# Batch 0's layer-norm statistics taken by VectorE, and the sums over the attention weights folded into one matrix product per chunk

## The chip, the cores and the metric

The kernel runs on one core of a Trainium2 chip. A core has a matrix engine (TensorE, "PE" in the profile, with its weight loads listed as "PEld"), a vector engine (VectorE, "DVE"), an activation engine (ScalarE, "ACT"), a general engine (GpSimd, "POOL") and a queue engine (SyncE, "SP"), each with its own instruction stream, which it works through in order; they wait for one another on semaphores. Sixteen DMA engines move data between the device memory and the on-chip memory; their transfers are issued from the SP, ACT and POOL streams. The metric is the device time of one execution in microseconds (us).

## The reference

The input `x` has 4 batches of 512 time steps (tokens), each with 128 x 64 = D = 8192 features. A first layer does linear attention, a convolution over the 128 frequencies, a causal convolution over time and a feed-forward network, each behind a layer norm over all 8192 features; a second layer does a spectral convolution over time. Only the beginning of the first layer matters here:

```python
xn = layernorm(x.reshape(b, t, d), ln_attn_g, ln_attn_b)
k = xn @ Wk
v = xn @ Wv
r = jax.nn.sigmoid(xn @ Wr)
decay = jnp.exp(-jnp.exp(w_decay))
kv = jnp.swapaxes(k * v, 0, 1)
...                                   # s = decay * s + kv, over time
attn = r * states @ Wo
x = x + attn.reshape(b, t, f, h)
xn = layernorm(x.reshape(b, t, d), ln_freq_g, ln_freq_b)...
```

`Wk`, `Wv`, `Wr` are 8192 x 64 and `Wo` is 64 x 8192. With g and b the weights of the first layer norm, mean m and inverse deviation s of a token, k = s (x (g Wk) - m (g . Wk)) + b . Wk: the product can run on raw x, and be corrected afterwards with the token's two statistics and with the column sums g . W and b . W of the weights. The statistics of the second layer norm, of x + attn, can also be had without a second pass over x: they need the 64 row sums of Wo (Wo times a vector of ones), the 64 x 64 matrix Wo Wo^T and the cross product x Wo^T.

## The kernel before

**Tiling.** x is held in two forms in device memory: feature-major `xt` (64 chunks of 128 features by 512 tokens) and token-major `x`. The 64 chunks are worked on in 32 pairs. `wkvr` holds, for each chunk, 128 rows of 256 numbers: the columns of Wk, Wv, Wr and Wo^T, 64 each.

**Stages.** For each batch the first layer runs `project` (k, v, r and x Wo^T summed over all chunks in PSUM), `scan` (corrections, the recurrence over time, and the second norm's statistics), `attend_and_convolve`, `convolve_time`, `open_feed` and `feed_forward`. The calls at the end of `layer0` set their order: `project(0)` runs alone, then `prepare()`, which folds constants, and then `in_turn` weaves two chains of stages into each other step by step (`scan(0)` and `attend_and_convolve(0)` with `project(1)` and `scan(1)`, and so on). TensorE's instructions stand in exactly this written order. For the other engines and for the SP stream, a scheduler that models the run chooses the order, and the instructions then wait for each other on semaphores; a stream never overtakes its own waiting instruction.

**`project`.** A pair takes one load of `wkvr` (line 333, 256 KB), one of `xt` (line 292, tile `xp`, 512 KB), a scaling of the three projection weights by g on VectorE (line 358, twice), and four products of 128 x 128 weights with 128 x 512 inputs (line 361). The two kinds of batch differ:

- Batch 0 (lines 336 to 348) has six small products per pair that add up g . W, b . W, Wo Wo^T and the sums of Wo (lines 341 to 343, with a column of ones that GpSimd writes at line 336). Its token statistics come from TensorE: ScalarE squares `xp` (line 345), and `add_up` (line 249) multiplies `xp` and its square, one pair late, by columns of ones. Its weights lie in the buffers called `x1` (three of them), which the attention uses later.
- Batches 1 to 3 (lines 351 to 355) load the same part of x a second time, token-major (512 KB per pair), and take the statistics from it with VectorE's `bn_stats`, two of 128 x 512 per pair. Weights and token-major data share the two buffers `wx`.

**`scan`.** Batch 0 turns the TensorE sums into columns (`finish`, lines 257 to 266), the other batches use `bn_aggr`. Then GpSimd computes the inverse deviation (`rsqrt`, lines 230 and 231), TensorE spreads mean and inverse deviation over the partitions (`rows`, line 239, copied by ScalarE at line 283), and a chain of VectorE work with single products between (lines 427 to 465) gives the gated state `rst`. Batch 0 also duplicates its weight sums over the two halves of the partitions (lines 402 to 418). In batch 0 the tile `kv` is one of the `x1` buffers.

**Buffers.** `xp` has three, `x1` three, `z` four, `wx` two. PSUM tiles (`a`, `c`, `m`, `p`, `s`) have one buffer each. `spare` is a small helper that allots one of these on-chip tiles by its tag.

Of the kernel before, what the change touches and what calls it, by code (L numbers as in the profile page):

```python
# [16 lines left out]
P = 128  # L17
# [62 lines left out]
def layer0(ctx, tc, dram, x, xt, vecs, wkvr, wo, wdec, wconv, fbias, w1, fb1, w2, fb2, x4):  # L80
# [209 lines left out]
    def load_x(b, i):  # L290
        xp = fr.tile([P, 2, SL], F32, tag="xp", name="xp")
        nc.sync.dma_start(xp, xt[b, 2 * i : 2 * i + 2].rearrange("c p t -> p c t"))
        return xp

    def c_bank():
        return two(ps_c, "c")
# [14 lines left out]
    free_s = [True]  # L311
    held = [False]


    def project(b):
        pa = two(ps_m, "m") if b == 1 else two(ps_a, "a")
        held[0] = b == 1
        if b == 0:
            psum_w = two(ps_m, "m")
            psum_q = ps_p.tile([P, SL], F32, tag="p", name="psum_q")  # L320
            st = ps_s.tile([P, SL], F32, tag="s", name="st")
        else:
            stt = rowp.tile([P, NT, NS, 6], F32, tag="stt", name="stt")
        waiting = None
        for i in range(NPR):
            first, last = i == 0, i == NPR - 1
            if b == 0:
                wq = two(fr, "x1")[:, :, 0 : 4 * S + 1]
            else:

                both = fr.tile([P, 2, 4 * S + SL], F32, tag="wx", name="both", bufs=2)
                wq, xk = both[:, :, 0 : 4 * S], both[:, :, 4 * S :]
            nc.sync.dma_start(wq[:, :, 0 : 4 * S], wkvr[2 * i : 2 * i + 2].rearrange("c p s -> p c s"))
            xp = load_x(b, i)
            if b == 0:
                nc.gpsimd.memset(wq[:, :, 4 * S :], 1.0)
                for j in range(2):
                    c = 2 * i + j
                    at = dict(start=c == 0, stop=c == NCH - 1)
                    w = wq[:, j, :]  # L340
                    nc.tensor.matmul(psum_w[:, 0, 0:2], lhsT=w[:, 0:P], rhs=vec[:, G1 : B1 + 1, c], **at)
                    nc.tensor.matmul(psum_w[0:S, 1, 0:2], lhsT=w[:, P : P + S], rhs=vec[:, G1 : B1 + 1, c], **at)
                    nc.tensor.matmul(psum_q[S:P, 0 : S + 1], lhsT=w[:, P + S : P + 2 * S], rhs=w[:, P + S :], **at)
                sq1 = bk.tile([P, 2, SL], F32, tag="sq", name="sq1")
                nc.scalar.activation(sq1, xp, AF.Square)
                if waiting is not None:
                    add_up(st, *waiting, i == 1, False)
                waiting = i, xp, sq1
            else:
                s, h = i // 2, i % 2 * 2  # L350
                nc.sync.dma_start(
                    xk, x[b, h * P : (h + 2) * P, s * SL : (s + 1) * SL].rearrange("(t p) d -> p t d", p=P)
                )
                for t in range(2):
                    nc.vector.bn_stats(stt[:, h + t, s, :], xk[:, t, :])  # L355
            for j in range(2):
                w = wq[:, j, 0 : 3 * S]
                nc.vector.tensor_scalar_mul(w, w, vec[:, G1, 2 * i + j : 2 * i + j + 1])  # L358
            for j in range(2):
                for k in range(2):  # L360
                    nc.tensor.matmul(  # L361
                        pa[:, k, :], lhsT=wq[:, j, k * P : (k + 1) * P], rhs=xp[:, j, :],
                        start=first and j == 0, stop=last and j == 1,
                    )
                yield 1.0
        if b == 0:
            add_up(st, *waiting, False, True)
        kvrg = rowp.tile([P, 2, SL], F32, tag="kvrg", name="kvrg")
        nc.scalar.copy(kvrg, pa)
        held[0] = False  # L370
        if b == 0:
            projected[b] = kvrg, st, psum_w, psum_q
        else:
            projected[b] = kvrg, stt


    def scan(b):
        kvrg, *left = projected.pop(b)
        bank = of_p if b == 1 else of_a
        rs, sq = cols("rs1"), cols("sq1")  # L380
        mean = cols("mean1")
        var = cols("var1")
        if b == 0:
            st, psum_w, psum_q = left
            m1, s1 = yield from finish(st, bank, 1)
            nc.vector.tensor_copy(mean, m1)
            nc.vector.tensor_copy(sq, s1)
            nc.vector.tensor_tensor(var, mean, mean, ALU.mult)
            nc.vector.tensor_tensor(var, sq, var, ALU.subtract)
        else:  # L390
            stt, = left
            mv = tiny.tile([P, NT, 2], F32, tag="mv", name="mv")
            for t in range(NT):
                nc.vector.bn_aggr(mv[:, t, :], stt[:, t, :, :])
            nc.vector.tensor_copy(mean, mv[:, :, 0])
            nc.vector.tensor_tensor(sq, mean, mean, ALU.mult)
            nc.vector.tensor_tensor(sq, sq, mv[:, :, 1], ALU.add)
            nc.vector.tensor_copy(var, mv[:, :, 1])
        rsqrt(rs, var)
        if b == 0:  # L400
            w_sb = const.tile([P, 2, 2], F32, name="w_sb")
            nc.vector.tensor_copy(w_sb[:, 0, :], psum_w[:, 0, 0:2])
            nc.vector.tensor_copy(w_sb[0:S, 1, :], psum_w[0:S, 1, 0:2])

            pw = bank()
            for q, (k, n) in enumerate(((0, P), (1, P), (0, S))):
                nc.tensor.matmul(
                    pw[:, 2 * q : 2 * q + 2], lhsT=sel[0:n, k, :, :].rearrange("p i s -> p (i s)"),
                    rhs=w_sb[0:n, q // 2, :], start=True, stop=True,
                )  # L410
            gw = sums["gw"] = const.tile([P, 3], F32, name="gw")
            bw = sums["bw"] = const.tile([P, 3], F32, name="bw")
# [3 lines left out]
            qo = sums["qo"] = const.tile([P, S + 1], F32, name="qo")  # L416
            nc.vector.tensor_copy(qo[S:P, 0:S], psum_q[S:P, 0:S])
            nc.vector.tensor_scalar_mul(qo[S:P, S:], psum_q[S:P, S : S + 1], 1.0 / D)
        gw, bw, qo = sums["gw"], sums["bw"], sums["qo"]
# [3 lines left out]
        else:  # L423
            kv = fr.tile([P, 2, 4 * S + SL], F32, tag="wx", name="kv", bufs=2)[:, :, 0:SL]
        for k in range(2):
# [40 lines left out]
        rs, mrs = moments(mean2, sq, 2)  # L466
        scanned[b] = rst, rs, mrs
        yield CHAIN


    def attend_and_convolve(b):
# [78 lines left out]
        carried[b] = moments(mean3, sq3, 3)  # L550

    def spare(tag, n):
        return fr.tile([P, 2, n], F32, tag=tag, name=tag, bufs={"z": 4, "wx": 2}.get(tag, 3))

# [437 lines left out]
def _inputs(x, i):  # L992
# [8 lines left out]
    vecs += [time_w[:, k] for k in range(3)]  # L1001
    wkvr = np.concatenate([i["Wk"], i["Wv"], i["Wr"], i["Wo"].T], axis=1)
    wo = i["Wo"][:, HALVES].reshape(S, NPR, 2, P).transpose(2, 0, 1, 3)
# [11 lines left out]
    for rows, parts in ((MODES, ("w_real", "w_imag")), (IMAG, ("w_imag", "w_real"))):  # L1015
# [7 lines left out]
        "vecs": np.stack([cols(v) for v in vecs], axis=1),  # L1023
        "wkvr": wkvr[HALVES].reshape(NCH, P, 4 * S),
        "wo": wo.reshape(P, NPR, P),
# [28 lines left out]
```

## Time and profile before

| | us |
|---|---|
| median of 3 runs | 3954.09 (3950.18 to 3962.51) |
| the profiled execution | 3956.46 |
| its span in the profile | 3954.4 |
| TensorE busy in the span | 3721.8 (94%) |
| VectorE, ScalarE, GpSimd busy | 2646.6, 1761.0, 580.8 |
| mean transfer rate over the span | 224 GB/s |
| end of `project(0)` in the trace | 186.74 |
| `project(1)`'s first product | 191.24 |

A row of costly groups reads: line, engine, operation, output<-input by the program's tile names, partitions x elements, count | busy us, mean ns of one | idle time of the engine just before them, and what ended it. A product of fp32 appears as two instructions. A row of the windows table reads: stretch, its length, busy time and number of instructions for PE, PEld, DVE, ACT and POOL, TensorE's granted clock as a share of full speed, the mean busy share of the DMA engines, and GB/s. A row of the timeline reads: start, length, engine, line, operation, tiles, shape, count, and in brackets the idle time before it and what ended that.

### The profile page before, as it was taken

What the parts mean: (1) busy time and instruction counts of PE and PEld (TensorE: products, weight loads), DVE (VectorE), ACT (ScalarE), POOL (GpSimd) and SP (SyncE); (2) the same over time, 40 slices, a digit from 0 to 9 for tenths busy, and PEclk for the clock granted to TensorE, in tenths of its full rate; (3) what the DMA queues carried; (4) which work ended last, traced back from release to release, by engine and by line L of the source; (5) the groups of instructions that cost most, each with busy time, mean ns of one, the idle gap of its engine ahead of it and who ended that gap; (6) DMA issues with size and microseconds to landing.
All of it is one profiled execution on the core that took longest, in us unless ns stands there. A gap on an engine that the chain in (4) does not pass through costs nothing. (4 is left out here: it accounts for less than half of the span.)

```text
span 3954.4 us, 45957 instructions
## 1 busy us (share of the span) xinstructions
PE 3721.8 (94%) x16463; PEld 1373.1 (35%) x16463; DVE 2646.6 (67%) x3430; ACT 1761.0 (45%) x2460; POOL 580.8 (15%) x1038
## 2 busy tenths in 40 slices
PE   9989989889999899999999988999989999999999
PEld 4433322223333222333322232333322653326533
DVE  1145559985555898655589989955549357783577
ACT  2113335545556555455556578877752210022100
POOL 0000002220000222000022222100014200142000
PEclk9989989999999999999989999999989999999999
DMA  5367637776664677767567767745549469895597
GB/s 173 126 224 262 231 127 242 249 254 228 232 234 149 232 258 247 247 221 236 172 209 255 258 218 257 244 160 179 182 155 306 163 196 297 297 303 176 186 294 268
DMA packets 417466, 884.49 MB, mean 224 GB/s; under 512 B 35352, under 2 KB 85720, under 8 KB 413144
## 3 DMA queue, kind: packets, MB, share of 16 engines
q1 hardware_dynamic: 334848, 605.12, 47.1%
q0 software_dynamic: 79872, 274.77, 19.3%
q8 instruction: 131, 2.15, 0.2%
q10 hardware_dynamic: 2520, 1.67, 0.1%
q14 instruction: 95, 0.78, 0.1%
HBM read 612.93 MB, written 268.50 MB: 223 GB/s over the span
## 5 line engine op out<-in xcount | busy, mean ns | idle before, releaser
L650 PE MATMUL pa<-mid,w_sb 128*64 128x512 f32 x2048 | 499.9, 609 | 49.5 <-DVE x4t L655 49.3
L643 ACT ACTIVATE mid<-m,fb_sb 128x1024 f32<-128x1024 f32 x256 | 284.9, 1113 | 294.8 <-PE m L639 294.2
L655 DVE SCALAR_TENSOR_TENSOR x4t<-pa,fb_sb,x 128x512 f32<-128x512 f32 x252 | 188.0, 746 | 254.2 <-PE pa L650 254.1
L639 PE MATMUL m<-x,w_sb 64*128 64x512 f32 x1008 | 289.8, 648 | 1.4 <-ACT mid L643 0.9
L589 DVE SCALAR_TENSOR_TENSOR to<-xh,vec,to 128x512 f32<-128x512 f32 x384 | 277.2, 746 | 10.7 <-issue 6.8
L643 ACT ACTIVATE mid<-c,fb_sb 128x1024 f32<-128x1024 f32 x256 | 283.2, 1106 | 0.6 <-PE c L639 0.6
L639 PE MATMUL c<-x,w_sb 64*128 64x512 f32 x1008 | 262.4, 594 | 1.3 <-ACT mid L643 1.3
L650 PEld LDWEIGHTS pa<-mid,w_sb 128*64 128x64 f32 x2048 | 125.0, 136 | 392.7 <-issue 227.5
L361 PE MATMUL a<-xp,both 128*128 128x512 f32 x512 | 244.8, 605 | 6.4 <-DVE both L358 5.9
L249 PE MATMUL st<-x,ones 128*32 128x512 f32 x512 | 204.2, 613 | 35.3 <-DVE x L525 35.2
L922 PE MATMUL b<-xin,avg_sb 128*128 128x512 f32 x512 | 230.9, 593 | 3.0 <-DVE xin L928 3.0
L899 ACT COPY two<-a 128x512 f32<-128x512 f32 x64 | 37.5, 585 | 424.1 <-PE a L894 424.1
L358 DVE TENSOR_SCALAR both<-both,vec 128x192 f32<-128x192 f32 x192 | 53.3, 316 | 258.5 <-DMA both<-in_wkvr 208.5
L928 DVE TENSOR_TENSOR xin<-b,pm 128x512 f32<-128x512 f32 x256 | 159.1, 684 | 95.4 <-PE b L925 80.5
L675 POOL DMA_DIRECT2D x<-ob x64 | 48.9, 765 | 1056.3 <-ACT ob L671 986.5
L616 ACT ACTIVATE kd<-kd,vec 128x512 f32<-128x512 f32 x256 | 193.6, 809 | 4.3 <-DVE kd L608 4.2
L528 ACT ACTIVATE sq<-x 128x1024 f32<-128x1024 f32 x128 | 134.6, 1051 | 135.6 <-DVE x L525 135.3
L249 PE MATMUL st<-sq,ones 128*32 128x512 f32 x640 | 172.2, 615 | 21.0 <-ACT sq L528 20.0
L825 DVE TENSOR_TENSOR uv<-xin 128x1024 f32<-128x1024 f32 x128 | 156.1, 1225 | 49.8 <-PE a L839 32.0
L355 DVE BATCH_NORM_STATS2 stt<-both 128x6 f32<-128x512 f32 x192 | 124.4, 685 | 92.7 <-DMA both<-in_x 91.8
L487 PE MATMUL a<-rst,wo_sb 64*128 64x512 f32 x512 | 153.5, 678 | 34.7 <-DVE x L489 33.6
L595 ACT ACTIVATE sq<-to 128x1024 f32<-128x1024 f32 x96 | 101.3, 1055 | 188.9 <-POOL xh L581 183.4
(242 smaller groups left out, 6804.3 us busy)
## 6 DMA issues: line engine op xcount, KB each, us to landing
xp<-in_xt SPq DMA_DIRECT2D x256, 512.0 KB
xin<-x SPq DMA_DIRECT2D x128, 1024.0 KB
kx<-x SPq DMA_DIRECT2D x224, 512.0 KB
x<-x POOLq DMA_DIRECT2D x128, 512.0 KB, 4.7
kh<-to SPq DMA_DIRECT2D x128, 512.0 KB
x<-ob POOLq DMA_DIRECT2D x64, 1024.0 KB, 6.7
out<-xin POOLq DMA_DIRECT2D x64, 1024.0 KB, 7.3
both<-in_x SPq DMA_DIRECT2D x96, 512.0 KB
```

The source lines that it names most:

```text
L249: nc.tensor.matmul(st[32 * q : 32 * q + 32, :], lhsT=ones, rhs=src[:, j, :], start=first, stop=last,)
L361: nc.tensor.matmul(pa[:, k, :], lhsT=wq[:, j, k * P : (k + 1) * P], rhs=xp[:, j, :], start=first and j == 0, stop=last and j == 1,)
L487: nc.tensor.matmul(at[:, j, :], lhsT=wo_sb[js, :], rhs=rst[js, :], start=True, stop=True)
L589: nc.vector.scalar_tensor_tensor(to[:, j, :], xh[:, j, k : SL + k], vec[:, w, c], to[:, j, :], ALU.mult, ALU.add)
L616: tc.keep_in_program_order(nc.scalar.activation(d[:, j, :], d[:, j, :], AF.Identity, bias=vec[:, B4, c], scale=vec[:, G4, c]))
L639: nc.tensor.matmul(pm[:, h, :], lhsT=w1_sb[hs, m * P : (m + 1) * P], rhs=x3[hs, :], start=True, stop=True)
L643: nc.scalar.activation(mid, pm, AF.Gelu_apprx_tanh, bias=fb1_sb[:, m : m + 1])
L650: nc.tensor.matmul(pa[h * H : (h + 1) * H, :], lhsT=w2_sb[:, m, :], rhs=mid[:, h, :], start=(m == 0), stop=(m == 1),)
L655: nc.vector.scalar_tensor_tensor(x4t, pa, fb2_sb, x3s[c // 2][:, c % 2, :], ALU.add, ALU.add)
L825: nc.vector.tensor_tensor(t, xin[:, 0:2, :], xin[:, 2:4, :], op)
L922: nc.tensor.matmul(po[j], lhsT=avg_sb[:, j, :], rhs=xin[:, j, :], start=True, stop=False)
L928: nc.vector.tensor_tensor(by_n(xin[:, j, :]), by_n(po[j]), by_c(pm[j % 2][:, j // 2, :]), ALU.add)
```

## The change

Batch 0 now takes its statistics as the other batches do, from a token-major load and `bn_stats`; the squaring on ScalarE and the `add_up` products of batch 0 are gone. The six small products per pair are replaced by two, one per chunk: `wkvr` gets g and b as two more columns (258 numbers per row, 1032 bytes), a column of ones follows on chip, and the product of the columns [Wo^T, g, b] (66) with the whole row [Wk, Wv, Wr, Wo^T, g, b, 1] (259) holds all the sums at once, in one PSUM tile. `scan` unpacks them: a copy of 66 x 259 out of PSUM, two small copies, three small products and one of 64 to 128 x 67. Batch 0's weights go to the `x1` buffers and its token-major data to the `z` buffers; so do `project(1)`'s until `scan(0)` has been written out (nine pairs), and `wx` is used from then on. Batches 1 to 3 still load 256 numbers per row, out of rows of 258. `scan(0)` has one step fewer to be woven (`finish` gave up its turn once).

```diff
@@ project
         if b == 0:
-            psum_w = two(ps_m, "m")
-            psum_q = ps_p.tile([P, SL], F32, tag="p", name="psum_q")
-            st = ps_s.tile([P, SL], F32, tag="s", name="st")
-        else:
-            stt = rowp.tile([P, NT, NS, 6], F32, tag="stt", name="stt")
-        waiting = None
+            psum_w = ps_p.tile([P, SL], F32, tag="p", name="psum_w")
+        stt = rowp.tile([P, NT, NS, 6], F32, tag="stt", name="stt")
         for i in range(NPR):
             first, last = i == 0, i == NPR - 1
+            if unscanned[0]:
+                wq, xk = two(fr, "x1")[:, :, 0 : 4 * S + 3], spare("z", SL)
+            else:
+                both = spare("wx", 4 * S + SL)
+                wq, xk = both[:, :, 0 : 4 * S], both[:, :, 4 * S :]
+            n = 4 * S + 2 * (b == 0)
+            nc.sync.dma_start(wq[:, :, 0 : n], wkvr[2 * i : 2 * i + 2, :, 0 : n].rearrange("c p s -> p c s"))
+            xp = load_x(b, i)
+            s, h = i // 2, i % 2 * 2
+            nc.sync.dma_start(
+                xk, x[b, h * P : (h + 2) * P, s * SL : (s + 1) * SL].rearrange("(t p) d -> p t d", p=P)
+            )
+            for t in range(2):
+                nc.vector.bn_stats(stt[:, h + t, s, :], xk[:, t, :])
             if b == 0:
-                wq = two(fr, "x1")[:, :, 0 : 4 * S + 1]
...
+                nc.gpsimd.memset(wq[:, :, n:], 1.0)
                 for j in range(2):
                     c = 2 * i + j
-                    at = dict(start=c == 0, stop=c == NCH - 1)
                     w = wq[:, j, :]
-                    nc.tensor.matmul(psum_w[:, 0, 0:2], lhsT=w[:, 0:P], rhs=vec[:, G1 : B1 + 1, c], **at)
-                    nc.tensor.matmul(psum_w[0:S, 1, 0:2], lhsT=w[:, P : P + S], rhs=vec[:, G1 : B1 + 1, c], **at)
-                    nc.tensor.matmul(psum_q[S:P, 0 : S + 1], lhsT=w[:, P + S : P + 2 * S], rhs=w[:, P + S :], **at)
-                sq1 = bk.tile([P, 2, SL], F32, tag="sq", name="sq1")
-                nc.scalar.activation(sq1, xp, AF.Square)
-                if waiting is not None:
-                    add_up(st, *waiting, i == 1, False)
-                waiting = i, xp, sq1
...
+                    nc.tensor.matmul(
+                        psum_w[0 : S + 2, 0 : 4 * S + 3], lhsT=w[:, 3 * S : 4 * S + 2], rhs=w,
+                        start=c == 0, stop=c == NCH - 1,
+                    )
@@ scan
-            m1, s1 = yield from finish(st, bank, 1)
...
+        mv = tiny.tile([P, NT, 2], F32, tag="mv", name="mv")
+        for t in range(NT):
+            nc.vector.bn_aggr(mv[:, t, :], stt[:, t, :, :])
...
+            w_sb = rowp.tile([P, SL], F32, tag="rg", name="w_sb")
+            nc.vector.tensor_copy(w_sb[0 : S + 2, 0 : 4 * S + 3], psum_w[0 : S + 2, 0 : 4 * S + 3])
+            twice = rowp.tile([P, SL], F32, tag="state", name="twice")
+            t4 = twice[S : S + 2, 0 : 6 * S].rearrange("p (q i s) -> p q i s", i=2, s=S)
+            for i in range(2):
+                nc.vector.tensor_copy(t4[:, :, i, :], w_sb[S : S + 2, 0 : 3 * S].rearrange("p (q s) -> p q s", s=S))
...
+                    pw[:, 2 * q : 2 * q + 2], lhsT=twice[S : S + 2, 2 * S * q : 2 * S * (q + 1)],
+                    rhs=ident[S : S + 2, S : S + 2], start=True, stop=True,
...
+            nc.tensor.matmul(
+                pq, lhsT=sel[0:S, 0, :, :].rearrange("p i s -> p (i s)"), rhs=w_sb[0:S, 3 * S : 4 * S + 3],
+                start=True, stop=True,
+            )
...
         scanned[b] = rst, rs, mrs
+        unscanned[0] = False
         yield CHAIN
@@ _inputs
-    wkvr = np.concatenate([i["Wk"], i["Wv"], i["Wr"], i["Wo"].T], axis=1)
+    wkvr = [i["Wk"], i["Wv"], i["Wr"], i["Wo"].T, i["ln_attn_g"][:, None], i["ln_attn_b"][:, None]]
...
-        "wkvr": wkvr[HALVES].reshape(NCH, P, 4 * S),
+        "wkvr": np.concatenate(wkvr, axis=1)[HALVES].reshape(NCH, P, 4 * S + 2),
```

## The prediction

> **What bounds the kernel now.** I read the page first (engines, slices), then the windows table over the first 300 us, the groups of the first 260 us with shapes apart, and the timelines of PE, DVE and SP there. TensorE carries the whole:
>
> ```profile
> span 3954.4 us, 45957 instructions
> PE 3721.8 (94%) x16463; PEld 1373.1 (35%) x16463; DVE 2646.6 (67%) x3430; ACT 1761.0 (45%) x2460; POOL 580.8 (15%) x1038
> PE   9989989889999899999999988999989999999999
> ```
>
> So TensorE time taken from the path comes off the end, unless another resource takes the place. The change acts in the first 260 us. The windows table there:
>
> ```profile
> 60.00:80.00 20.00, 20.00 (x98) 9.59 (x96) 1.92 (x6) 3.62 (x4) 0.41 (x4) 1.00 0.48 145
> ...
> 191.24:212.58 21.34, 19.56 (x41) 8.00 (x41) 7.04 (x22) 0.00 (x0) 0.00 (x0) 0.92 0.71 236
> 212.58:224.04 11.46, 9.23 (x31) 5.81 (x30) 4.24 (x15) 0.58 (x1) 1.28 (x2) 0.70 0.42 146
> ...
> 205.00:210.00 5.00, 3.46 (x8) 1.25 (x7) 1.84 (x4) 0.00 (x0) 0.00 (x0) 1.00 1.00 329
> ```
>
> `project(0)` (60 to 80): PE never idle at full clock, DVE under 2 of 20 us, DMA half used. The next rows are `project(1)` with `scan(0)`: PE waits and its clock falls. The last shows the DMA engines full at 329 GB/s with exactly the three kinds of load that the change gives to batch 0. One pair of `project(0)` in PE's timeline, then the groups:
>
> ```profile
> 23.61 0.28 PE L341 MATMUL m<-vec,x 128*128 128x2 f32 x2
> 24.66 0.62 PE L249 MATMUL st<-xp,ones 128*32 128x512 f32 x1
> 25.66 3.70 PE L361 MATMUL a<-xp,x 128*128 128x512 f32 x8
> 29.20 0.28 PE L341 MATMUL m<-vec,x 128*128 128x2 f32 x2
> ```
>
> ```profile
> L345 ACT ACTIVATE sq<-xp 128x1024 f32<-128x1024 f32 x32 | 33.8, 1055 | 133.0 <-PE st L249 133.0
> L358 DVE TENSOR_SCALAR x<-x,vec 128x192 f32<-128x192 f32 x64 | 20.5, 320 | 147.8 <-PE m L342 147.8
> L355 DVE BATCH_NORM_STATS2 stt<-both 128x6 f32<-128x512 f32 x24 | 15.6, 686 | 10.9 <-DMA both<-in_x 10.9
> ```
>
> A pair lasts 5.59 us (23.61 to 29.20): small products 1.05, statistics 1.00, projections 3.54. ScalarE and DVE only wait for PE.
>
> **What the Trainium skill says.** "TensorE: Matmul & The Clock Gate", section "Back-to-back issue gap": a product costs time in proportion to its moving columns. The trace agrees: eight 512-column instructions start every 0.427 us (start to start in PEld's rows of the timeline). The same page, "Part 1: The HAM clock gate": after about 3.4 us idle the clock halves, and about 3.4 us of activity restore it; here the mean is 0.70 in 212 to 224. "DMA: Bandwidth & Descriptors", "Specifications": about 358 GB/s of device memory per core; here 329 at share 1.00, and 340 at 0.97 in 200 to 205.
>
> **The change part by part.**
>
> *Project(0), TensorE.* Gone: 1.05 + 1.00. New: two products of 259 columns, each two instructions of 259/512 x 0.427 = 0.216 us: 0.86. New wait: `add_up` used to stand between the small products and the projections, and hid VectorE's scaling of the weights; now the scaling is exposed. The first chunk's product has been issued after 0.43 us, its result is out 0.17 later (a 512-column instruction lasts 0.593 against the 0.427 spacing), scaling is 0.32, release 0.05: 0.97 against 0.86, so 0.11 us of waiting. Pair: 3.54 + 0.86 + 0.11 = 4.51. The new product's price is not in the trace; below is 0.43 per pair (half of mine), above 1.71 (if it cost as 512 columns). I take proportion.
>
> *Project(0), VectorE.* Two `bn_stats` of 0.686 plus 0.64 scaling: 2.0 of 4.5 us, hidden under the projections. In the built order they stand between one pair's scalings and the next's: if token-major data is late, the next scaling waits behind it, and PE with it. ScalarE's 33.8 us of squares were not on the path: worth nothing.
>
> *Project(0), DMA.* A pair brings 0.264 + 0.524 + 0.524 = 1.31 MB instead of 0.79. In the built SP order 38 token-major loads precede the end, six for `project(1)`: 32 x 0.788 + 38 x 0.524 = 45.1 MB, with constants 46.2, or 1.44 MB per pair. At 329 GB/s that is 4.39 us; at 317 (the 149 GB/s at share 0.47 of 12 to 181 us, scaled to full) 4.56. PE and DMA are thus level. SP's three issues cost 0.37 + 0.37 + 0.47 = 1.2 us, hidden; three weight and `xp` buffers and four `z` keep over 2 MB asked for. Rows of 1032 bytes are unpriced: nothing at the low end, at the high end double the weights' time, 0.8 us per pair. I take a period of 4.60. The first pair needs its cold 7.5 us as now (4.9 to 12.4), plus 1.0 for a fuller start: 12.4 + 1.0 + 31 x 4.60 = 156.0 against 186.74. **Minus 30.7.** `prepare` (4.5 us) moves along unchanged; its DVE work now has one pair's `bn_stats` ahead (1.3 us), under PE's 2.8 us of products.
>
> *Project(1) and scan(0).* Now:
>
> ```profile
> 191.24 12.33 PE L361 MATMUL m<-xp,both 128*128 128x512 f32 x24
> 203.81 3.70 PE L361 MATMUL m<-xp,both 128*128 128x512 f32 x8 [0.24 <-DVE both L358]
> 209.05 3.70 PE L361 MATMUL m<-xp,both 128*128 128x512 f32 x8 [1.53 <-DVE both L358]
> ...
> 216.68 2.08 PE L239 MATMUL a<-ident,rs 128*128 128x128 f32 x8 [1.97 <-POOL rs L231]
> 218.55 5.65 PE L361 MATMUL m<-xp,both 128*128 128x512 f32 x8
> ```
>
> Five pairs take 21.3 us, since two `wx` buffers make loads late; three `x1` buffers and z data already there give 5 x 3.46 + 1.5 cold = 18.8: minus 2.5. The statistics chain (212.58 to 216.68, 4.1 us) ends earlier now, before PE arrives, since `bn_aggr` and `rsqrt` stand before `project(0)`'s end; 0.6 us of unpacking remain: minus 3.5. Without this stall the cold pair after it (5.5 us) runs at 3.5: minus 2. The wait for L431 (1.6 us) goes: minus 1.6. Added: SP issues the seventh pair's weights only behind an `xp` load that waits for the sixth pair, so PE waits about 3.5 us (a load took 196.63 to 199.50, 2.9 us, and 0.85 of other work covers; the `xp` ahead adds 1.5). The ninth pair's weights take the buffer of `kv`, and so wait for the recurrence; their scaling stands before `rst` in DVE's order, so `rst` is as late as now (about 3.4 us after the recurrence against 3.1), but less project work lies beside it: plus 2.5. Sum -3.6; I book **minus 4**, from -10 (loads earlier than I think) to +5 (both stalls cold: about 1.7 us each, and more).
>
> *After that* PE's order and the other queues' are nearly the same as before, shifted by a step: nothing. Batches 1 to 3 read rows out of 1032-byte strides; their stages run DMA at 0.5 to 0.8, which hides it.
>
> Sum 3954.4 - 34.7 = 3919.7 for the span; this execution's own time lay 2.1 above its span, and the median 0.3 below the span, so I predict 3919 for the median.
>
> **Rivals.** (1) *DMA holds project(0) at 5.1 us per pair* (about 280 GB/s, as the unpriced rows or the reads of two forms of x would do): 13.4 + 31 x 5.1 = 171.5, minus 15.2 - 4: 3935. For: demand is 97% of what was seen at best. Against: 329 at share 1.00 was this mix. (2) *Scan(0) loses what it gained*, +5 from both late loads with a cold clock: 3954 - 30.7 + 5 = 3928. (3) *The one product does not get cheaper*: 1.71 per pair, so 3.54 + 1.71 + 0.11 = 5.36, and 13.4 + 166.2 = 179.6: minus 7 - 4: 3943. Against: shorter products last less everywhere in the trace (0.24 for 2 columns, 0.593 for 512). (4) *Slower*: token-major loads late, `bn_stats` before the next scaling, PE waits in every pair: one loop in `project(0)`, that gets slower than before from (190.7 - 13.4)/31 = 5.72 us per pair, or 252 GB/s, on. At 220 GB/s: 6.5 per pair, 214.9, plus 28 - 4: 3978. Against it: rates of 300 and more wherever loads queue.
>
> **Chances.** Forecast 0.58 (3909 to 3927), (1) 0.18, (2) 0.11, (3) 0.05, (4) 0.08. The range for 8 in 10 runs from 3904 (the gains of the scan doubled, DMA at 340) to 3938, over (1) and (2). A change within 0.3% (12 us) can't be told from none. Faster 0.90, same 0.02, slower 0.08.
>
> **What would show it.** In the profile after: `psum_w` products 128 in number with spacing about 0.22 us; pairs of 4.5 to 4.7 us; DMA share 0.9 or more in the first 150 us with about 310 GB/s; `project(1)`'s first product near 160; PE idle before the seventh pair and before `rst`'s product; everything later the same, 35 us earlier. I am wrong if PE waits for `bn_stats` or for token-major loads in every pair, if the clock falls in `project(0)`, or if a later stage gives time back.

## The result

The changed kernel takes 3906.18 us (median of 4 runs, 3897.05 to 3909.18) against 3953.41 for the kernel before (4 runs): ratio 0.9873, 95% interval 0.9849 to 0.9897. It is faster by 47 us; the prediction was 3919, faster by 35. The median lies below the forecast's 3909 to 3927 and inside the wider 3904 to 3938. The profiled execution took 3909.18. In later executions the same code gave 3904.64 (5 runs, ratio 0.9879, 0.9858 to 0.9901).

The page of the changed kernel, the lines that answer to those of before:

```profile
span 3907.4 us, 44936 instructions
PE 3679.3 (94%) x15945; PEld 1344.5 (34%) x15945; DVE 2686.3 (69%) x3498; ACT 1726.6 (44%) x2427; POOL 582.5 (15%) x1038
PE   9999998899999898999998888999989999999999
```

TensorE has 518 instructions and 42.5 us of work less, and still sets the end at 94%. VectorE has 40 us more. The windows of `project(0)`:

```profile
60.00:80.00 20.00, 20.00 (x54) 8.80 (x53) 10.08 (x20) 0.00 (x0) 0.41 (x4) 1.00 0.94 317
...
120.00:140.00 20.00, 17.72 (x43) 7.54 (x42) 9.99 (x24) 0.00 (x0) 1.70 (x5) 0.91 0.81 262
```

VectorE went from 2 to 10 of 20 us and the DMA engines from 0.48 to 0.94, as forecast. But the second row has TensorE idle for 2.3 of 20 us, at a mean clock of 0.91: a stall. TensorE's timeline shows the normal pair, from one `psum_w` product to the next (first three lines), that stall, and three later waits:

```profile
16.06 1.04 PE L349 MATMUL psum_w<-x 128*66 128x259 f32 x4
17.08 3.70 PE L358 MATMUL a<-xp,x 128*128 128x512 f32 x8
20.61 1.04 PE L349 MATMUL psum_w<-x 128*66 128x259 f32 x4
...
130.61 5.40 PE L358 MATMUL a<-xp,x 128*128 128x512 f32 x8 [2.28 <-DVE x L355]
...
195.67 2.75 PE L358 MATMUL m<-xp,x 128*128 128x512 f32 x4 [3.59 <-DVE x L355]
...
207.02 1.97 PE L445 MATMUL a<-rst,qo 64*64 64x512 f32 x2 [2.13 <-DVE rst L440]
...
478.32 1.07 PE L445 MATMUL p<-rst,qo 64*64 64x512 f32 x2 [2.02 <-DVE rst L440]
```

A pair takes 4.55 us instead of 5.59. The waits at 195.67 and 207.02 are the two that the prediction names in `scan(0)`. The last line lies in a stage for which the prediction booked nothing: it is the product of `scan(1)`'s gated state.

Where the 47 us went. I cut each trace at three of TensorE's starts: `project(1)`'s first product, batch 0's first attention product, and batch 1's. In each cell: length, in brackets TensorE's idle time and its clock loss (busy time times one minus the granted clock, summed over the clock records), us.

```
                          start to        to batch 0's     to batch 1's       the rest
                          project(1)      attention        attention
before                    191.2 (6, 0)    64.9 (8, 6)      308.3 (15, 16)     3390.0
changed                   163.7 (11, 2)   62.4 (7, 8)      296.0 (10, 7)      3385.3
changed, second trace     164.2 (11, 2)   58.7 (7, 4)      295.1 (9, 7)       3384.6
gain, first / second      27.5 / 27.0     2.5 / 6.2        12.3 / 13.2        4.7 / 5.4
predicted gain            30.7            4                0                  0
```

The first two columns together came near the forecast. The third is the surprise: 12 to 13 us in a stage that I had called "nearly the same". It contains `scan(1)`. Here is the kernel before, TensorE's and then VectorE's timeline around `scan(1)`'s gated state:

```profile
511.85 1.96 PE L453 MATMUL p<-rst,qo 64*64 64x512 f32 x2 [5.90 <-DVE rst L448]
```

```profile
506.82 0.68 DVE L441 TENSOR_TENSOR rg<-rg,rm 128x512 f32<-128x512 f32 x1
509.46 1.29 DVE L355 BATCH_NORM_STATS2 stt<-both 128x6 f32<-128x512 f32 x2 [1.97 <-DMA both<-in_x]
510.66 0.53 DVE L358 TENSOR_SCALAR both<-both,vec 128x192 f32<-128x192 f32 x2
511.11 0.69 DVE L448 TENSOR_TENSOR rst<-rg,state 128x512 f32<-128x512 f32 x1
```

`rg` and `state` are done by 507.5, yet `rst` starts at 511.11: ahead of it in VectorE's stream stand the `bn_stats` of a pair of a later batch, waiting for their load, and that pair's scaling. In the changed kernel's VectorE timeline nothing of the sort lies between:

```profile
474.20 1.22 DVE L482 TENSOR_TENSOR x<-a,xp 128x1024 f32<-128x1024 f32 x1
475.34 1.22 DVE L438 TENSOR_TENSOR_SCAN state<-decb,wx 128x512 f32<-128x512 f32 x1
476.47 1.20 DVE L486 TENSOR_TENSOR z<-x,rm 128x1024 f32<-128x1024 f32 x1
477.58 0.69 DVE L440 TENSOR_TENSOR rst<-rg,state 128x512 f32<-128x512 f32 x1
```

Windows over that whole stage, before (256 to 564 us) and changed (226 to 522): the mean clock rises from 0.94 to 0.98.

```profile
256.00:564.00 308.00, 293.46 (x1245) 90.82 (x1244) 166.59 (x211) 98.52 (x138) 26.10 (x36) 0.94 0.64 216
```

```profile
226.00:522.00 296.00, 286.37 (x1249) 89.95 (x1248) 165.81 (x213) 98.56 (x138) 26.09 (x36) 0.98 0.68 227
```

What could have reordered VectorE there? The suspects are the step that `scan(0)` no longer yields, the nine pairs moved to other buffers, and the single product. The experiments take them one at a time. Their second question is what made `project(0)` 3 us slower than forecast.

### The profile page after: what moved, and what is told of

It is laid out like the page before. It is cut to its first block, busy times and chain, and to the rows that moved or that the text cites. A ratio compares the mean times of both kernels' runs of the same rounds, so it can differ in the third digit from the quotient of the medians.

```text
span 3907.4 us, 44936 instructions
## 1 busy us (share of the span) xinstructions
PE 3679.3 (94%) x15945; PEld 1344.5 (34%) x15945; DVE 2686.3 (69%) x3498; ACT 1726.6 (44%) x2427; POOL 582.5 (15%) x1038
## 5 line engine op out<-in xcount | busy, mean ns | idle before, releaser
L358 PE MATMUL a<-xp,wx 128*128 128x512 f32 x512 | 241.0, 597 | 6.4 <-DVE wx L355 5.9
L355 DVE TENSOR_SCALAR wx<-wx,vec 128x192 f32<-128x192 f32 x174 | 48.3, 317 | 241.2 <-DMA wx<-in_wkvr 217.4
L480 PE MATMUL a<-rst,wo_sb 64*128 64x512 f32 x512 | 153.3, 673 | 34.4 <-DVE x L482 33.3
L575 ACT ACTIVATE to<-xh,tb_all,vec 128x512 f32<-128x512 f32 x192 | 149.4, 803 | 77.4 <-DVE xh L572 64.0
L794 DVE COPY xf<-b 128x256 f32<-128x256 f32 x128 | 54.4, 425 | 183.4 <-PE b L858 182.8
```

The costliest lines, as they stand in the source:

```text
L358: nc.tensor.matmul(pa[:, k, :], lhsT=wq[:, j, k * P : (k + 1) * P], rhs=xp[:, j, :], start=first and j == 0, stop=last and j == 1,)
L480: nc.tensor.matmul(at[:, j, :], lhsT=wo_sb[js, :], rhs=rst[js, :], start=True, stop=True)
```

## The experiments

The medians are of 4 or 5 executions (20 or more where the text says so), each compared with executions of the kernel before on the same chip. The runs were made on two chips, so between runs the ratios are to be compared and not the medians. One kernel's executions spread over 8 to 27 us, so besides the median I read the stages from the trace, which is of one execution.

### The lost step, put back into the changed kernel

```diff
         rsqrt(rs, var)
         if b == 0:
+            yield CHAIN
             psum_w, = left
```

> The changed kernel with the one step of scan(0) put back at which batch 0's scan used to give up its turn; no work differs. Theory (weave): losing that step shifted the weaving of attend_and_convolve(0) against project(1) and scan(1), so that the recurrence of scan(1) no longer stands behind a bn_stats that waits for a load; this run is 6 to 11 us slower than the changed kernel (3912 to 3917), with the wait of TensorE for rst in scan(1) at 5 to 6 us instead of 2.0 and a cold clock after it. Rival (earlier start): the gain at scan(1) came with everything being earlier, and stays: within 3 us of the changed kernel.

Measured: 3903.84, ratio 0.9882 (0.9863 to 0.9900), so no slower than the changed kernel. The wait came back as the theory says; the waits of the stage to batch 1's attention:

```profile
PE p L446 <- DVE rst L441: 5.8, 1, 5.8
```

That stage grew to 300.5 us (from 296.0 and 295.1), less than half of the 12 to 13 us that it had gained, but the one before it shrank to 53.2 (from 62.4 and 58.7). The trace is of the fastest of the five executions, 3892.92. In that stage this kernel has no wait for the seventh pair's scaling, since its SP stream issues that pair's weights ahead of the loads that wait, and the wait for `rst` at 201.41 is 1.15. So one step moves two things in opposite directions, and the 6 to 11 us that I expected in the total did not come. The place of the effect held.

### The step taken from the kernel before

```diff
-    def finish(st, bank, tag):
+    def finish(st, bank, tag, turn=True):
...
         nc.scalar.copy(s_sb, st)
-        yield CHAIN
+        if turn:
+            yield CHAIN
...
-            m1, s1 = yield from finish(st, bank, 1)
+            m1, s1 = yield from finish(st, bank, 1, False)
```

> The kernel before with one change: the scan of batch 0 doesn't give up its turn after the copy of the sums. Theory (weave): 6 to 11 us faster than before (3942 to 3947), with the wait for rst in scan(1) at about 2 us instead of 5.9. Rival (earlier start): within 3 us of before.

Measured: 3938.81 (20 executions) against 3950.38 (25): ratio 0.9972, 0.9962 to 0.9982, so 11 us (7 to 15) for a change that adds or removes no arithmetic. The waits:

```profile
PE p L454 <- DVE rst L449: 2.0, 1, 2.0
```

The stage to batch 1's attention took 299.3 instead of 308.3. (The trace is of the slowest of the 20 executions, 3958.21: the wait and the stage are to be read from it, not the total.) This is the clearest of the runs: in the kernel before, the step alone brings the gain.

### All of project(1) in its old buffers

```diff
-            if unscanned[0]:
+            if b == 0:
```

> The changed kernel, but project(1) uses the wx buffers from its first pair on; x1 and z serve batch 0 alone. Theory (the moved loads are worth nothing net): project(1)'s first five pairs take about 21 us instead of 18.5, but the seventh pair's late weights (3.6 us) and the ninth's behind kv go, with their cold clock; 3902 to 3910. Rival (the buffers carry the gain beyond the prediction): 3914 or more.

Measured: 3906.07, ratio 0.9890 (0.9873 to 0.9906). The moved loads are worth nothing net, and they are not what reordered `scan(1)`: the wait stays at 2.0 and the stage at 295.1. Inside the total things moved: the wait of 3.6 us for the seventh pair is gone, `scan(0)`'s wait for `rst` grew from 2.13 to 4.17, and `project(1)` starts at 160.4, with 3.1 instead of 4.8 us of waits in `project(0)`. Why these are smaller is not shown.

### VectorE's statistics alone

In the kernel before, batch 0's statistics from token-major loads in the `z` buffers; six small products and all steps kept.

```diff
+            if b == 0:
+                xk = spare("z", SL)
+            s, h = i // 2, i % 2 * 2
+            nc.sync.dma_start(
+                xk, x[b, h * P : (h + 2) * P, s * SL : (s + 1) * SL].rearrange("(t p) d -> p t d", p=P)
+            )
+            for t in range(2):
+                nc.vector.bn_stats(stt[:, h + t, s, :], xk[:, t, :])
...
-                sq1 = bk.tile([P, 2, SL], F32, tag="sq", name="sq1")
-                nc.scalar.activation(sq1, xp, AF.Square)
-                if waiting is not None:
-                    add_up(st, *waiting, i == 1, False)
-                waiting = i, xp, sq1
...
```

> The kernel before with the statistics of batch 0 from token-major x on VectorE (in the z buffers), the six small products kept, project(1) in wx from the start, the scan's steps as before. Theory (the statistics carry project(0)): pair 3.54 + 1.05 + 0.1 = 4.7 us, level with the 4.77 that the changed kernel really took, so project(0) ends at 157 to 162 as there, and the whole is 3915 to 3926 (no shift of the weave). Rival (the single product matters as much): pairs over 4.9 us, project(0) ends after 164, 3930 or more.

Measured: 3907.52, ratio 0.9895 (0.9878 to 0.9912): below what either theory gave, and level with the whole change. Its `project(0)` is better than the changed kernel's: every pair after the first takes 4.59 us, and `project(1)` starts at 160.1. TensorE in `project(0)` and the waits of the stage with `scan(1)`:

```profile
40.00:60.00 20.00, 20.00 (x93) 11.10 (x91) 7.56 (x17) 0.00 (x0) 0.51 (x5) 1.00 0.86 287
60.00:80.00 20.00, 20.00 (x88) 10.90 (x88) 8.78 (x20) 0.00 (x0) 0.41 (x4) 1.00 0.84 279
```

```profile
PE p L441 <- DVE rst L436: 6.0, 1, 6.0
```

TensorE has no idle time from pair to pair in `project(0)`; the old wait for `rst` is there, and the stage takes 307.0. So starting 31 us earlier does not remove that wait. Neither theory had the 7 us that the stage to batch 0's attention gained (57.8 instead of 64.9).

### The single product alone

In the kernel before, six products replaced by two, with the wider `wkvr`; statistics by `add_up` and buffers as before.

```diff
-                    nc.tensor.matmul(psum_w[:, 0, 0:2], lhsT=w[:, 0:P], rhs=vec[:, G1 : B1 + 1, c], **at)
...
+                    nc.tensor.matmul(psum_w[0 : S + 2, 0 : 4 * S + 3], lhsT=w[:, 3 * S : 4 * S + 2], rhs=w, **at)
```

> The kernel before with the single product per chunk alone; statistics by TensorE, buffers and steps as before. Theory (price in proportion to the 259 columns): pair 5.59 - 1.05 + 0.86 = 5.40 us, with the scaling still hidden behind the statistics products; project(0) ends 5 to 7 us earlier (180 to 182), the total 3942 to 3947. Rival (the product costs like 512 columns): pair 6.2 us, 20 us slower.

Measured: 3945.12 (22 executions) against 3948.76: ratio 0.9990, 0.9982 to 0.9998. A pair takes 5.50 instead of 5.59, and `project(1)` starts 3.6 us earlier, less than the 5 to 7 expected. TensorE's timeline gives the reason:

```profile
66.12 1.04 PE L341 MATMUL psum_w<-x 128*66 128x259 f32 x4
67.09 0.62 PE L249 MATMUL st<-xp,ones 128*32 128x512 f32 x1
```

The four instructions start 0.218 us apart, as forecast, but they take 0.97 together and not 0.86, since the product after them starts 0.31 after the last. The six small ones took 1.05. The single product is not what reordered `scan(1)` either: its wait for `rst` is 6.04 here, and the stage takes 307.8.

### Without batch 0's token-major loads

```diff
...
-            nc.sync.dma_start(
+            if b > 0:
+              nc.sync.dma_start(
                 xk, x[b, h * P : (h + 2) * P, s * SL : (s + 1) * SL].rearrange("(t p) d -> p t d", p=P)
             )
...
-                nc.vector.bn_stats(stt[:, h + t, s, :], xk[:, t, :])
+                nc.vector.bn_stats(stt[:, h + t, s, :], (xk if b > 0 else xp)[:, t, :])
```

This leaves out 16.8 MB of loads (32 of 0.524); batch 0's statistics are then taken over the elements of the feature-major tile, and are not those of the tokens.

> The changed kernel without batch 0's token-major loads: its bn_stats read xp, the feature-major tile, instead, so the statistics of batch 0 are left wrong and only their work is kept. Theory (DMA and TensorE level in project(0)): without the third load no pair waits, the pair takes 4.55 us throughout (TensorE's own 3.54 + 0.86 + 0.15) and project(0) ends at 152 to 153.5 instead of 159.2; total 5 to 8 us faster. Rival (VectorE's bn_stats or the exposed scaling make the pairs long): still 4.7 us or more on average, project(0) ends after 156.

Measured: 3901.99, ratio 0.9883 (0.9862 to 0.9904), but `project(1)` starts at 166.5: later. Windows and waits of its `project(0)`:

```profile
60.00:80.00 20.00, 19.38 (x54) 8.37 (x51) 8.48 (x18) 0.00 (x0) 0.51 (x5) 1.00 0.48 158
80.00:100.00 20.00, 19.01 (x51) 8.26 (x51) 7.70 (x19) 0.00 (x0) 0.41 (x4) 1.00 0.49 161
```

```profile
PE a L360 <- DVE x L357: 8.3, 16, 1.1
```

With half the traffic TensorE waits more often: 16 times for the scaling against 5, in front of which `bn_stats` now waits for `xp`. The theory of the run, that no pair would wait, did not hold: a bandwidth limit is not needed to make these waits. The run is no clean test of it, though, since the loads that `bn_stats` needs have changed too.

### kv in a buffer of its own

```diff
-            kv = two(fr, "x1")
+            kv = rowp.tile([P, 2, SL], F32, tag="rm4", name="kv")
```

> The changed kernel with kv of scan(0) in a buffer of its own (the rows of a later stage) instead of one of the three x1 buffers. In the built order the seventh pair's weights of project(1) are then asked for before the loads that wait, and the ninth pair's no longer wait for the recurrence. Theory (the late weights in scan(0)): TensorE's 3.6 us wait before the seventh pair and the half clock after it go, and from project(1)'s first product to the first attention product takes 53 to 56 us instead of 62.4; total 3896 to 3901. Rival (the chain of VectorE work bounds this stretch, not the loads): the wait moves to rst, the stretch stays at 60 or more, total within 3 us of the changed kernel.

Measured: 3898.68, ratio 0.9865 (0.9842 to 0.9889). The stage to batch 0's attention took 54.1 instead of 62.4 and 58.7, as expected. The first lines of that stage's waits, changed kernel and then this one:

```profile
PE m L358 <- DVE x L355: 3.6, 1, 3.6
PE a L445 <- DVE rst L440: 2.1, 1, 2.1
```

```profile
PE a L445 <- DVE rst L440: 2.1, 1, 2.1
PE c L199 <- DVE both L197: 0.8, 1, 0.8
```

The seventh pair's wait is gone, and the wait for `rst` stayed as it was. The late weights cost the changed kernel some 5 to 8 us in this stage.

### The changed kernel again

> The changed kernel once more, for a second trace and a tighter median. Theory (clock phase): stages after attend_and_convolve(0) differ between two traces of one and the same kernel by 5 to 15 us, through how much of the time the clock is halved, while project(0) ends within 3 us of 159 and the wait for rst in scan(1) is 2.0 again; median 3900 to 3910. Rival: the trace repeats stage by stage within 2 us, and differences between kernels in the late stages are real.

Measured: 3904.64. The second trace repeats the first stage within 0.5 us and the third within 0.9, but differs by 3.7 in the one between them. The rest differs by 0.7. So the theory of this run, that the late stages of one kernel's traces differ by 5 to 15 us, was not borne out by this pair. The "rest" is the same work in all kernels, and by the traces it ran from 3374.9 us (the first experiment, clock loss there 52) to 3399.7 (the second, clock loss 70). The clock can be only a part of that: the kernel with `project(1)` in its old buffers took 3383.9 at a clock loss of 52 as well.

### VectorE's order in project(0) held fixed

TensorE waits for a scaling in five pairs (not six) of the changed kernel's `project(0)`. In front of four of these scalings VectorE's built order has two pairs' `bn_stats` one after the other. One of them in its timeline:

```profile
48.56 0.76 DVE L355 TENSOR_SCALAR x<-x,vec 128x192 f32<-128x192 f32 x2 [1.92 <-PE psum_w L349]
51.52 2.61 DVE L342 BATCH_NORM_STATS2 stt<-z 128x6 f32<-128x512 f32 x4 [2.21 <-DMA z<-in_x]
54.04 0.53 DVE L355 TENSOR_SCALAR x<-x,vec 128x192 f32<-128x192 f32 x2
```

The scaling was due at about 53.1 and came at 54.04; TensorE waited 0.90. The fifth, the stall at 130.61, is the longest and has another cause:

```profile
127.30 1.02 DVE L377 BATCH_NORM_AGGREGATE mv<-stt 128x2 f32<-128x96 f32 x2
128.23 1.22 DVE L342 BATCH_NORM_STATS2 stt<-z 128x6 f32<-128x512 f32 x2
129.37 1.02 DVE L377 BATCH_NORM_AGGREGATE mv<-stt 128x2 f32<-128x96 f32 x2
130.30 0.25 DVE L355 TENSOR_SCALAR x<-x,vec 128x192 f32<-128x192 f32 x1
```

Here `scan(0)`'s `bn_aggr` and the last pair's `bn_stats` stand in front of the 27th pair's scaling. The first three wait for nothing: the last pair's token-major data had landed while the 27th pair was being worked on. The edit keeps scaling and `bn_stats` of batch 0 in the order of the pairs, and with that `bn_aggr`, which needs all of the `bn_stats`, comes later too:

```diff
-            for t in range(2):
-                nc.vector.bn_stats(stt[:, h + t, s, :], xk[:, t, :])
...
-                nc.vector.tensor_scalar_mul(w, w, vec[:, G1, 2 * i + j : 2 * i + j + 1])
+                sc = nc.vector.tensor_scalar_mul(w, w, vec[:, G1, 2 * i + j : 2 * i + j + 1])
+                if b == 0:
+                    tc.keep_in_program_order(sc)
+            for t in range(2):
+                bs = nc.vector.bn_stats(stt[:, h + t, s, :], xk[:, t, :])
+                if b == 0:
+                    tc.keep_in_program_order(bs)
```

> Batch 0's scalings and bn_stats kept on VectorE in the order of the pairs (scaling of a pair, then its bn_stats); loads and arithmetic as in the changed kernel. Theory 'order': what project(0) lost against a flat 4.55 us per pair were 6.6 us in six pairs, where two pairs' bn_stats stood one after the other in front of a scaling; now all pairs take 4.55 (the cold first one apart), the projections of project(0) end at 152 to 154 (159.4 in the changed kernel), the wait of the projections for the scaling is under 1 us after the first pairs, and the whole is 3896 to 3900. Rival 'transfers': the DMA engines hold the average at 4.77 per pair; the waits only go to other pairs, project(0) ends at 158 to 160, and the whole is 3902 to 3907.

Measured: 3894.81 (4 executions, 3887.43 to 3906.88), ratio 0.9862 (0.9842 to 0.9883). All pairs but the first and the last take 4.55. TensorE's timeline, then windows:

```profile
4.81 1.96 PE L347 MATMUL psum_w<-x 128*66 128x259 f32 x4 [4.81 <-DMA x<-in_wkvr]
9.52 5.50 PE L362 MATMUL a<-xp,x 128*128 128x512 f32 x8 [2.75 <-DMA x<-in_wkvr]
```

```profile
12.00:40.00 28.00, 28.00 (x73) 12.12 (x72) 11.36 (x26) 0.00 (x0) 0.62 (x6) 1.00 1.02 350
40.00:60.00 20.00, 20.00 (x54) 8.79 (x53) 8.08 (x19) 0.00 (x0) 0.41 (x4) 1.00 0.96 310
60.00:80.00 20.00, 20.00 (x55) 8.73 (x54) 8.03 (x19) 0.00 (x0) 0.51 (x5) 1.00 0.97 323
```

TensorE is never idle in these stretches, at 4.55 us per pair with the same loads, so "transfers" falls: the DMA engines carried this rate, at shares of 0.91 to 1.02 up to 140 us. The end of `project(0)` came at 156.6, not 152 to 154. The fixed order also put the first scaling behind VectorE's work on constants, and the first projections started at 9.52 instead of 7.00. (The idle time of 2.75 is put down to the weights' load, but these had been there since 4.81, when the product on them began; VectorE's scaling ran at 9.15.) The second pair began at 14.86 instead of 11.51; without these 3.35 us the end would lie at 153.3, an estimate from the two traces. `project(1)` starts at 161.0 instead of 163.7 and 164.2.

The same kernel once more:

> The same kernel again, for a second trace of it: the pairs' spacing, the end of project(0) and the waits repeat within 1 us by either theory.

One execution, 3902.37: its pairs are 4.55 again, and `project(0)` ends at 157.9. That is 1.2 later and not within 1, since the second pair began at 16.44 instead of 14.86.

### Both, the fixed order and kv in its own buffer

> The kept order and kv in a buffer of its own (as in the run with kv alone, 3898.7). Theory: the two gains lie in different stretches and add: 3890 to 3896, first product of project(1) at 156 to 158, first attention product 53 to 56 later. Rival 'transfers', or that the stalls only move: 3897 to 3901.

Measured: 3886.95 (5 executions, 3885.07 to 3897.44), ratio 0.9844 (0.9826 to 0.9862). The gains add: the three stages take 161.3, 54.0 and 289.5. `project(1)` starts later than the 156 to 158 expected, for the second pair begins at 15.52 here too, not at 11.51; the total is lower than expected. This version beats the kernel before clearly. It was not timed side by side with the changed kernel; by the ratios it is 0.0029 and 0.0035 of 3950, or 11 and 14 us, ahead of the changed kernel's two medians, with intervals that overlap or just touch.

### The step taken from the kernel with VectorE's statistics

```diff
-        if b == 0:
-            yield CHAIN
```

> The kernel with VectorE's statistics and the six small products, now with the step of scan(0) left out too. Theory: the lost step is worth 8 to 12 us here as in the kernel before, since it decides whether scan(1)'s gated state stands behind another pair's bn_stats: wait for it 2.0 (not 6.0), and 3896 to 3900 against 3907.5 with the step. Rival: the single product, not the step, shortened the attention stage of batch 0, or the step's gain was that kernel's alone: 3904 to 3911, wait 5.8 to 6.0.

Measured: 3902.67 (5 executions, 3890.54 to 3911.58), ratio 0.9879 (0.9858 to 0.9900). The wait:

```profile
PE p L439 <- DVE rst L434: 2.0, 1, 2.0
```

The stage to batch 1's attention fell from 307.0 to 292.6. Of these 14 us the ratios show only 6, with overlapping intervals: in the traces the rest took 9.6 more (3386.3 against 3376.7), at 59 us of clock loss against 51. So the mechanism is confirmed, but not its size in the total.

## Why the prediction was right or wrong

**Right: direction, and the main term.** Taking the statistics off TensorE carries the gain: VectorE's statistics alone, without the rest of the change, gave ratio 0.9895. A pair was forecast at 4.51 for TensorE alone and takes 4.55; products spaced 0.22 are there, and in an even pair VectorE's work is hidden. Of the parts, `project(0)` gained 3 us less than forecast, the stage with `scan(1)` 12 us more, and 5 us came in the rest. The reasons that the prediction gave for the low end of its wide range (the gains of `scan(0)` doubled, DMA at 340) are not what brought the result there.

**Mis-sized: "I take a period of 4.60".** The mean from the second pair on is (159.22 - 11.51)/31 = 4.77. It is no period at all: 4.55 flat, with 6.6 us more in five pairs. I had named one mechanism, "if token-major data is late, the next scaling waits behind it, and PE with it", but priced it only in the rival that is slower, in every pair. It fits four of the five pairs, with 2.6 us in all. The other 4.0 us fall on the pair at 130 us, and the prediction had them nowhere: `bn_aggr` "before `project(0)`'s end" was booked as a gain for `scan(0)` alone, yet there it stands in front of a scaling, for 2.28 us of waiting and, behind it, 3.42 us at half clock, which cost 1.7. Both are VectorE's order and not the DMA rate: with the order fixed, the same loads run at 4.55. Against that the first pair was 1.9 us better than "1.0 for a fuller start" allowed (11.51 against 13.4); that is luck in part, since with the same `project(0)` other traces have 11.24 to 12.90. Predicted 30.7 to the end of `project(0)`; measured 186.74 - 159.22 = 27.5.

**About right: the single product.** I set the gain against the six at 1.05 - 0.86 - 0.11 = 0.08 us per pair. Alone, with the statistics' products as cover, it gains 0.09 (the 0.19 expected of that run were wrong); beside VectorE's statistics 4.59 becomes 4.55. So it is worth 1 to 3 us over 32 pairs, and in the changed kernel it came with the order that cost 6.6. The kernel with VectorE's statistics and without the step, but with the six products and the old buffers, has a ratio of 0.9879 against the changed kernel's 0.9873 and 0.9879, so in the whole the product's worth can't be seen. The price in proportion to columns, which the prediction took from the Trainium skill, held for 259 against 512 (0.218 against 0.427 us); it does not hold for the six products of 2 and 65 columns, which took 1.05 us together where proportion gives 0.23, by an estimate from the 0.427.

**Project(1) and scan(0): about right.** Booked minus 4, measured minus 2.5 and minus 6.2. The seventh pair waits 3.59 (about 3.5 forecast), the unpacking's own wait is 0.7 (0.6). The link from `kv` to a late `rst` was wrong: with `kv` elsewhere that wait is still 2.13. What `kv` costs is the seventh pair's wait: with it in another buffer that wait is gone and the stage took 54.1.

**The step that failed: "*After that* PE's order and the other queues' are nearly the same as before, shifted by a step: nothing."** TensorE's order is nearly the same; VectorE's is not. In the kernel before, `scan(1)`'s `rst` stands behind another pair's `bn_stats`, which wait for a load; in the changed kernel it does not. TensorE's wait goes from 5.9 to 2.0, and the stage loses 5 us of idle time and 9 of clock loss: 12 to 13 us in both traces. That the lost step does it is shown by the kernel before without the step, 11 us faster, wait 2.0, and twice more by the wait: 6.0 to 2.0 where the step is taken from the kernel with VectorE's statistics, 2.0 to 5.8 where it is put back into the changed kernel. Over all 14 traces the four kernels with the step have waits of 5.8 to 6.0 and stages of 300.5 to 308.3 us, the ten traces without it waits of 2.0 and stages of 289.5 to 299.3. Had I booked the 11 us and used the measured 27.5, the sum would be 3954.4 - 27.5 - 4 - 11 = 3911.9. The 11 us belong to the kernel before, though. In the changed kernel the step put back cost this stage 5 us and the total nothing, since the stage in front of it gained 5 to 9; so the cause of the gain in this stage is shown, but not that the total's miss hangs on the step alone.

**The rivals.** Rival 1 (the DMA holds `project(0)` at 5.1) is refuted: 4.77 on average, and with the order fixed 4.55 with TensorE never idle. Rival 2 took the late loads for +5; they cost about that, but inside a net gain. Rival 3 (the product no cheaper per column) is refuted by the spacing of 0.218. Rival 4 came in small, as said.

**Left open.** The rest of the program ran 4.7 and 5.4 us shorter in the changed kernel's two traces than in the one of before. The work there is the same, and two traces of one kernel, that with the fixed order, differ by 4.0 in it. Yet the three kernels with TensorE's statistics have 3390.0 to 3399.7 there, and the eleven traces with VectorE's 3374.9 to 3387.5, so that a part may be real; no run shows what it would be. Nor is it shown why the scheduler's order puts `bn_stats` ahead of `rst` with the step and not without it.

## What to carry to other kernels

A change of one yielded step, with no arithmetic in it, was worth 11 us here: after any edit to a woven program compare every engine's built order near each product that waits alone, and not TensorE's only. In an in-order stream, an instruction that is not urgent, above all one that waits for a load, must not stand ahead of one that TensorE waits for; where a scheduler put it there, fixing the order of two kinds of instruction was enough to give even pairs. And when a stage's average period exceeds the sum of its parts, look at the single periods before calling it bandwidth: here even pairs with a stall in five of them came from the order, and each stall has to be read by itself.

## What the runs showed of the hardware that I had not expected

- The DMA engines moved 350 GB/s for 28 us (12 to 40 us with the fixed order, share 1.02), where I had taken 329 as full from a 5 us window. "DMA: Bandwidth & Descriptors", "Specifications", in the Trainium skill has about 358; the run comes close to it.
- The prediction took from the Trainium skill that the clock halves after about 3.4 us idle. Here shorter waits were enough: behind the wait of 2.28 us at 130.61 the clock was at 0.50 from 131.90 to 135.32, and in the second trace it fell in the same way behind a wait of 2.54.
- Executions of one kernel with the same instruction order differ by 8 to 27 us, and the traces' total clock loss runs from 61 to 89 us over all these kernels. "TensorE: Matmul & The Clock Gate", "Part 1: The HAM clock gate", says that the window in which activity is counted runs free of the kernel, and that the same kernel therefore has more or fewer slow products from run to run. The two traces of the changed kernel agree: its wait for `rst` in `scan(0)` is 2.13 us in one and 2.12 in the other, both end near 207 us, and the windows behind it are

```profile
207.00:213.83 6.83, 6.81 (x8) 2.47 (x9) 1.38 (x2) 0.00 (x0) 0.00 (x0) 0.50 0.01 2
```

```profile
207.00:213.83 6.83, 6.73 (x27) 3.71 (x28) 1.55 (x5) 0.00 (x0) 0.00 (x0) 1.00 0.21 77
```

So nearly equal waits were followed by 6.8 us at half clock in one execution and by full clock in the other, and in this kernel 4 or 5 executions don't settle a difference of 5 us.
